# A circulant correlation in a real Fourier basis instead of by skews, a halved last load, and root arithmetic moved to GpSimd

## Chip, cores and metric

The kernel runs on one core of one Trainium2 chip. The metric is device time of one execution in microseconds (us), lower is better. TensorE is called PE below, VectorE DVE, ScalarE ACT, GpSimd POOL and SyncE SP; in the code they are `PE`, `V`, `A`, `G`, `SP`.

## What is computed

Two stages: a cross attention that works by autocorrelation, and a gated FFN whose operands are rounded to FP4 in blocks of 16. Input is x and a context, both 64 x 128 x 256 f32.

```python
def reference(x, ctx, Wq, bq, Wout, bout, w_gate, w_up, w_down):
    h = layernorm(x)
    q, k, v = ((t @ Wq + bq).transpose(0, 2, 1) for t in (h, ctx, ctx))   # 64 x 16 x 128
    corr = real(ifft(fft(q) * conj(fft(k)))).mean((0, 1))                 # 128 lags
    w, lag = top_k(corr, 12); w = softmax(w)
    R3 = sum(w[i] * roll(v, -lag[i], -1) for i in range(12))
    R = broadcast(R3, 16 heads).reshape(64, 128, 256)
    x = x + R @ Wout + bout
    h = layernorm(x)
    g, u = fp4_linear(h, w_gate), fp4_linear(h, w_up)                     # 704 wide
    return x + fp4_linear(silu(g) * u, w_down)
```

`fp4_linear` scales each block of 16 by its largest absolute value over 6, rounds to the FP4 grid and multiplies the rounded operands. As R3 is broadcast over 16 heads and then reshaped, `R @ Wout` has only 4 different blocks of 128 rows, which serve 64 row tiles of x. They are called O[0] to O[3]; each has a 257th column, the mean of its row, for the layernorm that follows.

## The kernel before

**Planner.** Instructions are not issued in the order of the code. `op(engine, cost, function, r=, w=, dl=, ...)` records an operation with what it reads and writes, a cost in ns and a due time `dl`; `Order.emit` works out one order for each engine's queue from the costs and the due times, and issues it. Due times are handed back from an operation to those it needs. The constants at L346 to L376 set the due times: `SLOT` is the length of one FFN tile (5425 ns), `LC` the number of slots by which the down products of a tile may follow its gate and up products, `LEAD` by how many slots the preparation of an x batch runs ahead, `TK`, `TC`, `TO`, `TG`, `TW` the due times of single steps.

**Phase 1 (to about 55 us).** One SP queue loads, in the order of the string `LOADS` (L373): weights, x transposed in sixteen 512 KB pieces (`xt`, into eight buffers that are reused), the context in eight 1 MB blocks (`ct`, five buffers), then Wout (`Wo`) and the bias (`Bo`, broadcast to 128 partitions). DVE and ACT round the FFN weights to FP4 and split each into a high and a low f16 part (`WgH`, `WgL`, `WdH`, `WdL`), transposed by DMA. PE projects x to `qT`, with the layernorm applied behind it, and each context block to `kT` (`pk`, L1053); k and v are the same. For each of the 16 blocks of 128 rows `pg` (L1076) adds kTᵀ qT, a 128 x 128 sum over all batches and channels. Filler products of the identity ("heating", L724) keep PE's clock up where it would stand still.

**From pg to O (54.7 to 66 us).** The correlation at a lag is the sum of a circular diagonal of pg. pg is copied twice side by side to `W` (L1091), and `skew` shifts row p by p in seven predicated copies, each for one bit of p, of W onto itself 64, 32, ... 1 columns to the left (L329 to L341).

A product with ones (L1365) then gives the correlation C, the same on all partitions. `max`, `match_replace`, `max`, `match_replace` (L1387 on) find the 12 largest, `E` (ACT) holds the exponentials, and a masked product gives the weights twice side by side in `M` with their sum `es`. A second skew makes `M` the circulant matrix of the weights. M times Wo (L1441) is `Wp`, divided by `es`; eight pairs of transposes (L1372) with a copy each turn kT into `Vn`, which is v with time on the partitions. For each of four g, three products (bias row, two of Vn and Wp, L1459) make O[g], copied by ACT (L1466). ACT also computes the row means of Wo and Bo, loads the table for Sqrt, and fills the constant end columns of the three h buffers (`least`, L1476).

**Phase 2, the FFN (73.6 us to the end).** There are 64 tiles in 16 x batches of four. `x_parts` (L424 to L651) prepares a batch: row mean `neg`, `cc` = x + O less its mean, squares with a sum (`junk`, L507), block maxima `am` (L517), the reciprocal root of the variance, scaling, rounding (`k`, on ACT) and a split into two f16 parts (`xhl`). From tile 8 on the addition of O to X is a DMA that adds, issued by POOL (L481), and the root is worked out by `roots` (L402 to L422), eleven DVE steps on 128 x 4 or 128 x 8 values: once each for batches 2 and 3, then once per two batches. The step at L550 (it writes `am`) reads the result. The first eight tiles take ACT's Sqrt. Tiles of x are transposed (`xT`) by PE for the first two batches and by DMA after.

`group_ops` (L1140 to L1341) runs one or two tiles: gate and up products `gu` (18 matmuls per tile, L1166), Silu `g` (ACT, L1172), `h` = gate times up (DVE, L1179), block maxima `hs` (DVE, L1189) and their reciprocal (`hr`), the wide product `z` (POOL, L1218; DVE for the first and the last two tiles), rounding `hk`, `hc` (ACT), `hl` (DVE, L1271), a DMA transpose to `hT`, down products `pd` (17 matmuls per tile, L1315 and L1317), the sum with X (L1334) and the output DMA. Before the FFN two of the `gu` accumulators are called `hot` and `pa`.

## Time and profile before

| what | us |
|---|---|
| median of three runs | 439.63 |
| lowest and highest of them | 439.36 and 443.25 |
| the profiled execution | 438.03 |
| its span in the profile | 435.9 |
| last context block waited for until | 51.20 |
| last `pg` product ends | 54.72 |
| first copy of O starts | 66.01 |
| first `gu` product of the FFN starts | 73.57 |
| last `pd` product ends | 432.55 |

The profiled execution is 2.13 us longer than its span, which counts from the first instruction to the last on the engines. The table of stretches gives what each engine did between those marks (columns: stretch, its length, then for each engine busy us and instructions; PEclk is the granted clock as a share of full speed, then the busy share of the DMA engines and GB/s):

```profile
0.00:20.00 20.00, 16.33 (x151) 12.08 (x152) 16.30 (x59) 9.24 (x10) 0.92 (x8) 1.00 0.89 339
20.00:54.72 34.72, 33.26 (x445) 21.38 (x441) 25.31 (x56) 27.22 (x40) 0.00 (x0) 1.00 1.05 389
54.72:73.57 18.85, 14.78 (x87) 11.07 (x87) 14.46 (x52) 10.63 (x36) 1.08 (x2) 1.00 1.07 289
73.57:129.28 55.71, 50.14 (x294) 28.10 (x294) 54.90 (x129) 46.03 (x95) 20.55 (x19) 1.00 0.54 114
129.28:432.55 303.27, 301.40 (x1976) 192.76 (x1976) 277.27 (x537) 193.06 (x307) 114.39 (x94) 1.00 0.67 146
```

Between 73.57 and 129.28 DVE is busy 54.90 of 55.71 us and PE 50.14; from there to 432.55 PE is busy 301.40 of 303.27. Instructions of an engine run in its queue's order, so one that waits holds all that stand behind it.

### The profile page before, as it was taken

The page shows a single profiled execution, that of the slowest core. Times are in us where ns is not written, and L with a number is a line of the kernel's source. Part 1 is how long each engine was busy: PE and PEld are TensorE (multiplying, and loading weights), DVE is VectorE, ACT ScalarE, POOL GpSimd, SP SyncE. Part 2 cuts the span into 40 slices and gives each one's busy share as a digit, 9 for nine tenths or more (in the row PEclk, how much of TensorE's full clock was granted, in tenths as well). Part 3 has the DMA queues.
Part 4 walks back from the last instruction along what each step waited for, and adds up shares of the span by engine and source line. Part 5 has one row for each costly group of instructions (what it writes and reads, how often), then busy time and mean ns, then how long its engine had stood idle before and what let it go on. Part 6 is the DMA issues. An engine that isn't in the chain of part 4 may idle for free.

```text
span 435.9 us, 7976 instructions
## 1 busy us (share of the span) xinstructions
PE 415.9 (95%) x2948; PEld 265.4 (61%) x2948; DVE 388.7 (89%) x832; ACT 286.2 (66%) x484; POOL 136.9 (31%) x121
## 2 busy tenths in 40 slices
PE   7999978889899999999999999999999999999996
PEld 6457655446555656566566666666665666566685
DVE  6999368999999999989999989999999999978872
ACT  2797547988596696467946794887579666464410
POOL 0000003044444264344444444454434222324100
PEclk9999999999999999999999999999999999999999
DMA  7999999253787588579767897687578615952362
GB/s 282 408 415 420 334 215 358 37 105 71 151 185 142 131 196 175 139 117 233 157 136 161 197 158 163 139 176 152 117 161 164 156 39 120 192 125 66 94 169 74
DMA packets 151495, 76.61 MB, mean 176 GB/s; under 512 B 134432, under 2 KB 141984, under 8 KB 150432
## 3 DMA queue, kind: packets, MB, share of 16 engines
q1 hardware_dynamic: 143968, 69.29, 59.5%
q0 software_dynamic: 7488, 6.82, 11.0%
q8 instruction: 23, 0.38, 0.4%
q14 instruction: 16, 0.13, 0.1%
HBM read 27.76 MB, written 8.39 MB: 83 GB/s over the span
## 4 chain that ended last, share of the span: by engine, by line
PE 61%; DVE 16%; DMA 9%; ACT 9%; issue 2%; SPq 1%; DVEq 0%; ACTq 0%
PE gu L1166 37%; PE pd L1315 14%; PE pd L1317 8%; DMA ct<-in_cx_dram 6%; DMA xt<-in_xt_dram 4%; DVE hs L1189 3%; DVE h L1179 2%; DVE hl L1271 2%; ACT junk L507 2%; ACT cc L497 2%; ACT g L1172 2%; DVE am L517 1%; ACT hk L1246 1%; ACT hc L1262 1%; DVE hr L1203 1%
## 5 line engine op out<-in xcount | busy, mean ns | idle before, releaser
L1166 PE MATMUL gu<-WgH,xT 128*128 128x512 f16 (+1 forms) x768 | 191.7, 361 | 5.5 <-ACT g L1172 1.5
L1166 PEld LDWEIGHTS <-xT 128*128 128x128 f16 x1152 | 112.4, 98 | 114.8 <-issue 4.5
L1218 POOL TENSOR_TENSOR h<-h,hr 128x704 f32<-128x704 f32 x61 | 92.8, 1521 | 199.0 <-DVE hr L1203 169.7
L1166 PE MATMUL gu<-WgL,xT 128*128 128x512 f16 (+1 forms) x384 | 107.4, 361 | 0.0
L1172 ACT ACTIVATE g<-gu,ug 128x704 f32<-128x704 f32 x64 | 53.6, 840 | 41.8 <-PE gu L1166 41.6
L1246 ACT ACTIVATE hk<-h,c_half 128x1408 int16<-128x1408 f32 (+1 forms) x34 | 47.4, 1394 | 37.3 <-POOL h L1218 34.5
L1189 DVE TENSOR_REDUCE hs<-h 128x44 f32<-128x792 f32 x64 | 66.7, 1042 | 2.1
L481 POOL DMA_DIRECT2D X<-O x52 | 45.7, 939 | 71.0 <-DMA X<-in_x_dram 71.0
L1179 DVE SCALAR_TENSOR_TENSOR h<-gu,uh,g 128x704 f32<-128x704 f32 x64 | 55.9, 874 | 5.0 <-ACT g L1172 3.2
L1262 ACT ACTIVATE hc<-hk,c_sub 128x1408 f16<-128x1408 int16 (+1 forms) x32 | 45.6, 1426 | 0.5
L1315 PE MATMUL pd<-WdH,hT 128*128 128x256 f16 x352 | 43.7, 273 | 1.2 <-DMA hT<-hl 1.2
L1315 PEld LDWEIGHTS <-hT 128*128 128x128 f16 x352 | 34.3, 98 | 9.5 <-DMA hT<-hl 1.6
L1334 DVE SCALAR_TENSOR_TENSOR X<-pd,ud,X 128x512 f32<-128x512 f32 (+1 forms) x34 | 24.3, 715 | 11.3 <-PE pd L1317 11.3
L497 ACT ACTIVATE cc<-X,neg 128x256 f32<-128x256 f32 x62 | 30.2, 497 | 3.6 <-DVE neg L459 2.9
L1271 DVE TENSOR_TENSOR hl<-hc,hsb 128x1408 f16<-128x1408 f16 (+1 forms) x34 | 28.7, 843 | 0.2
L1271 DVE TENSOR_TENSOR hl<-hc,hsl 128x1408 f16<-128x1408 f16 (+1 forms) x34 | 28.6, 841 | 0.0
L1203 DVE RECIPROCAL hr<-hs 128x44 f32<-128x44 f32 x64 | 26.8, 419 | 0.2
L507 ACT ACTIVATE junk<-cc 128x256 bf16<-128x256 f32 x64 | 25.9, 405 | 1.0 <-DVE cc L470 0.8
L1317 PE MATMUL pd<-WdL,hT 128*128 128x256 f16 x192 | 26.2, 273 | 0.0
L1232 ACT ACTIVATE hsb<-hs 128x176 bf16<-128x176 f32 (+1 forms) x34 | 11.4, 334 | 19.8 <-DVE hs L1189 19.8
L912 ACT ACTIVATE xsq<-xt,shift 128x1024 f32<-128x1024 f32 x16 | 18.1, 1148 | 9.5 <-DVE shift L908 7.0
L584 DVE TENSOR_TENSOR cc<-cc,rz 128x256 f32<-128x256 f32 x64 | 23.3, 418 | 0.1
(215 smaller groups left out, 532.9 us busy)
## 6 DMA issues: line engine op xcount, KB each, us to landing
xt<-in_xt_dram SPq DMA_DIRECT2D x16, 512.0 KB, 8.1
ct<-in_cx_dram SPq DMA_DIRECT2D x8, 1024.0 KB, 11.5
X<-in_x_dram SPq DMA_DIRECT2D x16, 512.0 KB, 4.5
out_dram<-X SPq DMA_DIRECT2D x30, 256.0 KB, 2.3
X<-O POOLq DMA_DIRECT2D x52, 128.0 KB, 2.8
Wg<-in_wgu_dram SPq DMA_DIRECT2D x2, 512.0 KB, 4.5
Wdn<-in_wd_dram SPq DMA_DIRECT2D x1, 704.0 KB, 9.6
hT<-hl SPq DMA_TRANSPOSE x32, 3.3
```

What stands on the lines that cost most here:

```text
L481: lambda i=i: G.dma_start(Xq.t[:, i0 + i], O[g][:, 0:D], accum_op=ALU.add),
L497: lambda i=i: A.activation(T["cc"].t[:, i], Xq.t[:, i0 + i], AF.Identity, bias=T["neg"].t[:, i : i + 1]),
L1166: PE.matmul(pg.t[:, c0:c1], src[:, b], w[:, k, c0:c1], start=(m == 0), stop=(m == 5))
L1172: lambda pg=pg, g=g: A.activation(g.t, pg.t[:, 0:NF], AF.Silu, scale=ug),
L1179: lambda pg=pg, g=g, i=i: V.scalar_tensor_tensor(B["h"].t[:, i, 0:NF], pg.t[:, NF:NG], uh, g.t, ALU.mult, ALU.mult),
L1189: lambda i=i: V.tensor_reduce(B["s"].t[:, i], B["h"].t[:, i].rearrange("p (jj b e) -> p b jj e", b=NB, e=2), AX.XY, ALU.max, apply_absolut ...
L1218: lambda i=i, zv=zv: (V if zv else G).tensor_tensor(per_block(B["h"].t[:, i, 0:NF], NB), per_block(B["h"].t[:, i, 0:NF], NB), spread(B["r" ...
L1246: lambda: A.activation(sub("k"), sub("h")[:, :, 0:NF], AF.Identity, bias=c_half, scale=24.0),
L1262: lambda: A.activation(flat("c"), flat("k"), AF.Identity, bias=c_sub, scale=SUB),
L1271: lambda e=e, part=part: V.tensor_tensor(B["hl"].t[:, 0:nt, e].rearrange("p t (jj n) -> p t jj n", jj=JJ), sub("c").rearrange("p t (jj n) ...
L1315: PE.matmul(pd, hT.t[:, b], WdH[:, :, b], start=(b == 0), stop=False)
L1317: PE.matmul(pd, hT.t[:, b], WdL[:, :, b], start=False, stop=(b == 5))
```

## The change

**Loads and layout.** The context is laid out on the host so that each half block is a run of its own; the last block is loaded as two halves (`c7a`, `c7b`). The bias is one row instead of 128 and is loaded before the context. The host no longer reverses rows of Wo.

**Fourier basis.** In phase 1 a real Fourier basis is computed: `four[:, 0]` and `four[:, 1]` hold cosine and sine of 2πfl/128 (f from the partition, l along the row), by a triangle wave and a polynomial; `four[:, 2]` is the basis B with cosines on partitions 0 to 64 and sines above, `four[:, 3]` its quarter-turned partner J. `wt` holds the weights of the frequencies. PE transposes B and J into `fourT`.

**From pg to O.** Both skews go. pg is copied once to W; the product T = B W (`fourT[:, 0]` as stationary) and two weighted sums along rows (`uv`) give the spectrum of the correlation, and two products with cosine and sine bring C back. `max` to weights stays, with the weights once in `wm`; two weighted sums (`wv`) give their spectrum. Beside that PE computes B and J times Wo (`spec`) and B times Vn (`Va`, copied by ACT). Wp is a combination of B Wo and J Wo with wv as scalars; O[g] = Vaᵀ Wp plus the bias row times `es`, and the copy to O[g] divides by `es`. kT is turned in four groups of four transposes instead of eight of two, all free to go once T is done (`VB = 0` makes them wait for T only). Row means of Wo and Bo go from ACT to DVE. The load of the Sqrt table moves from behind E to behind the first Va copy and the ACT part of Wp.

**Elsewhere.** The `least` fills and nine of the eleven root steps go to POOL (fourteen steps there, for lack of a fused form). `LC`, `LEAD` and one due time of the first xT copies change, and with them the planned order. The two DMA transposes of the gate weights wait for the second half of the last context block.

```diff
...
+    four = res.tile([P, 4, P], F32, name="four")
+    fourT = res.tile([P, 2, P], F32, name="fourT")
...
-    for k in range(7):
-        V.tensor_single_scalar(bits_i[:, k : k + 1], pidx, 64 >> k, ALU.bitwise_and)
-    V.tensor_copy(bits, bits_i)
+    pf, sine, cosine, fr, wt, wt2, nwt = (const.tile([P, 1], F32, name=n) for n in ("pf", "sine", "cosine", "fr", "wt", "wt2", "nwt"))
+    V.tensor_copy(pf, pidx)
+    V.tensor_scalar(sine, pidx, 64.0, None, ALU.is_gt)
+    V.tensor_scalar(cosine, sine, -1.0, 1.0, ALU.mult, ALU.add)
+    V.scalar_tensor_tensor(fr, sine, -64.0, pf, ALU.mult, ALU.add)
+    V.tensor_scalar(wt, fr, 0.0, -1.0 / P, ALU.is_equal, ALU.mult)
+    V.tensor_scalar(wt2, fr, 64.0, -1.0 / P, ALU.is_equal, ALU.mult)
+    V.scalar_tensor_tensor(wt, wt, 2.0 / P, wt2, ALU.add, ALU.add)
+    V.tensor_scalar(nwt, wt, -1.0, None, ALU.mult)
...
-    def skew(W, key, **kw):
...
-    LC = 4.5
+    LC = 5.5
...
+    VB = 0
+    TF = 49000.0
...
+    GT = 180.0
...
-    LEAD = (0.5, 0.5)
+    LEAD = (3.0, 0.0)
...
+    LOADS = "wq bq wg0 wg1 x0 wg2 x1 x2 x3 wd x4 x5 x6 x7 x8 x9 x10 x11 x12 x13 x14 x15 bo c0 c1 c2 c3 c4 c5 c6 c7a c7b wo"
...
-        op("V", 75, lambda: V.tensor_tensor(t, y, y, ALU.mult), r=[by], w=[bt])
-        op("V", 75, lambda: V.tensor_tensor(t, t, v, ALU.mult), r=[bv], w=[bt])
...
+        op("G", GT, lambda: G.tensor_tensor(t, y, y, ALU.mult), r=[by], w=[bt], port=False)
+        op("G", GT, lambda: G.tensor_tensor(t, t, v, ALU.mult), r=[bv], w=[bt], port=False)
+        op("G", GT, lambda: G.tensor_scalar(p, t, -4.2, None, ALU.add), r=[bt], w=[bp], port=False)
+        op("G", GT, lambda: G.tensor_tensor(p, p, t, ALU.mult), r=[bt], w=[bp], port=False)
+        op("G", GT, lambda: G.tensor_scalar(p, p, 7.0, None, ALU.add), r=[], w=[bp], port=False)
+        op("G", GT, lambda: G.tensor_tensor(p, p, t, ALU.mult), r=[bt], w=[bp], port=False)
+        op("G", GT, lambda: G.tensor_scalar(p, p, -7.0, None, ALU.add), r=[], w=[bp], port=False)
+        op("G", GT, lambda: G.tensor_tensor(y, p, y, ALU.mult), r=[bp], w=[by], port=False)
+        op("G", GT, lambda: G.tensor_tensor(t, y, y, ALU.mult), r=[by], w=[bt], port=False)
+        op("G", GT, lambda: G.tensor_tensor(t, t, v, ALU.mult), r=[bv], w=[bt], port=False)
+        op("G", GT, lambda: G.tensor_scalar(t, t, -0.5 / 3.2**2, 1.5, ALU.mult, ALU.add), r=[], w=[bt], port=False)
+        op("G", GT, lambda: G.tensor_tensor(y, t, y, ALU.mult), r=[bt], w=[by], port=False)
+        op("G", GT, lambda: G.tensor_tensor(t, v, y, ALU.mult), r=[bv, by], w=[bt], port=False)
+        op("G", GT, lambda: G.tensor_scalar(t, t, TINY / 4.0 / -3.2, None, ALU.mult), r=[], w=[bt], port=False)
...
-                op("V" if fast else "A", 420 if fast else 590, f_x, r=[pt], w=[(T["xT"], i)], dl=due - 300, port=False)
+                op("V" if fast else "A", 420 if fast else 590, f_x, r=[pt], w=[(T["xT"], i)], dl=due - (4300 if fast else 300), port=False)
...
-            "bo": (400, ["Bo"], lambda: SP.dma_start(Bo[:, 0:D], bo.partition_broadcast(P))),
+            "bo": (60, ["Bo"], lambda: SP.dma_start(Bo[:, 0:D], bo)),
...
+                    lambda j=j, b=b: SP.dma_start(cts[j].t[:, b], cx[j, b]),
...
+        mrow = W
...
+        op("G", 300, lambda: G.iota(ang(), pattern=[[0, 2], [1, P]], base=0, channel_multiplier=0), w=[(scr, "ang")])
+        for k in range(2):
+            op("V", 170, lambda k=k: V.tensor_scalar(ang()[:, k], ang()[:, k], fr, 96.0 * k, ALU.mult, ALU.add), w=[(scr, "ang")], dl=TF)
+        op("V", 300, lambda: V.tensor_single_scalar(ang(), ang(), 127, ALU.bitwise_and), w=[(scr, "ang")])
+        op("V", 220, lambda: V.tensor_scalar(tri(), ang(), -1.0 / 64.0, 1.0, ALU.mult, ALU.add), r=[(scr, "ang")], w=[(scr, "tri")])
+        op("V", 330, lambda: V.scalar_tensor_tensor(tri(), tri(), -1.0, tri(), ALU.mult, ALU.max), w=[(scr, "tri")])
+        op("V", 220, lambda: V.tensor_scalar(tri(), tri(), -0.5, None, ALU.add), w=[(scr, "tri")])
+        op("V", 330, lambda: V.tensor_tensor(tri2(), tri(), tri(), ALU.mult), r=[(scr, "tri")], w=[(scr, "tri2")])
+        op("V", 220, lambda: V.tensor_scalar(poly(), tri2(), SIN[4], SIN[3], ALU.mult, ALU.add), r=[(scr, "tri2")], w=[(scr, "poly")])
+        op("V", 330, lambda: V.tensor_tensor(poly(), poly(), tri2(), ALU.mult), r=[(scr, "tri2")], w=[(scr, "poly")])
+        for k in (2, 1):
+            op("V", 330, lambda k=k: V.scalar_tensor_tensor(poly(), poly(), SIN[k], tri2(), ALU.add, ALU.mult), r=[(scr, "tri2")], w=[(scr, "poly")])
+        op("V", 330, lambda: V.scalar_tensor_tensor(four[:, 0:2], poly(), SIN[0], tri(), ALU.add, ALU.mult), r=[(scr, "poly"), (scr, "tri")], w=["four"])
+        for k in range(2):
+            op("V", 130, lambda k=k: V.tensor_scalar(tri()[:, k], four[:, 1 - k], sine, None, ALU.mult), r=["four"], w=[(scr, "tri")])
+            op(
+                "V",
+                200,
+                lambda k=k: V.scalar_tensor_tensor(four[:, 2 + k], four[:, k], cosine, tri()[:, k], ALU.mult, (ALU.add, ALU.subtract)[k]),
+                r=["four", (scr, "tri")],
+                w=["base"],
+            )
+        op("V", 330, lambda: V.tensor_reduce(Bo[:, D : D + 1], Bo[:, 0:D], AX.X, ALU.add), w=["Bo"], dl=TF)
+        op("V", 75, lambda: V.tensor_scalar(Bo[:, D : D + 1], Bo[:, D : D + 1], 1.0 / D, None, ALU.mult), w=["Bo"], dl=TF)
+        pf_t = r_m.new()
+
+        def f_four():
+            for k in range(2):
+                PE.transpose(pf_t.t[:, k * P : (k + 1) * P], four[:, 2 + k], ident)
+
+        op("PE", 300, f_four, r=["base"], w=[pf_t], dl=TC - 1500.0)
+        op("A", 350, lambda: A.copy(fourT.rearrange("p k n -> p (k n)"), pf_t.t[:, 0 : 2 * P]), r=[pf_t], w=["fourT"], dl=TC - 1000.0)
+        op("V", 220, lambda: V.tensor_copy(W, pg), r=["pg"], w=["W", "mrow"], dl=TC + 4000.0)
...
-    skew(W, "W")
...
-    sums = op("PE", 220, lambda: PE.matmul(hot.t[:, 512 : 512 + P], ones, W[:, 0:P], start=True, stop=True), r=["W"], w=[pc])
...
+    T_op = op("PE", 270, lambda: PE.matmul(C(), fourT[:, 0], W, start=True, stop=True), r=["W", "fourT"], w=[pc])
+    uv_ops = []
+    for k in range(2):
+        uv_op = op(
+            "V",
+            280,
+            lambda k=k: V.scalar_tensor_tensor(jk, C(), wt, four[:, 2 + k], ALU.mult, ALU.mult, accum_out=uv[:, k : k + 1]),
+            r=[pc, "base"],
+            w=["jk", ("uv", k)],
+        )
+        uv_ops.append(uv_op)
+
+    def f_c():
+        for k in range(2):
+            PE.matmul(C(), uv[:, k : k + 1].broadcast_to([P, P]), four[:, k], start=(k == 0), stop=(k == 1))
+
+    sums = op("PE", 540, f_c, r=[("uv", 0), ("uv", 1), "four"], w=[pc])
+    op("V", 600, lambda: V.tensor_reduce(Wo[:, :, D : D + 1], Wo[:, :, 0:D], AX.X, ALU.add), w=["Wo"], after=uv_ops)
+    op("V", 75, lambda: V.tensor_scalar(Wo[:, :, D : D + 1], Wo[:, :, D : D + 1], 1.0 / D, None, ALU.mult), w=["Wo"])
+    pv3 = Q["pd"].new()
+    for j in range(4):
+        key, pv = ((pa, j), pa.t[:, 512 * j : 512 * j + 512]) if j < 3 else (pv3, pv3.t)
 
         def f_v(j=j, pv=pv):
-            for b in range(2):
-                PE.transpose(pv.t[:, b * P : (b + 1) * P], kT[:, 2 * j + b], ident)
-
-        op("PE", 220, f_v, r=[("kT", 2 * j), ("kT", 2 * j + 1)], w=[pv], after=after)
+            for b in range(4):
+                PE.transpose(pv[:, b * P : (b + 1) * P], kT[:, 4 * j + b], ident)
...
+        op("PE", 600, f_v, r=[("kT", 4 * j + b) for b in range(4)], w=[key], after=(T_op,) if j >= VB else ())
...
+    pb1 = Q["pd"].new()
+    spec = {
+        ("B", 0): ((hot, "b0"), lambda: hot.t[:, 512 + P : 512 + P + D + 1]),
+        ("J", 0): ((hot, 2), lambda: hot.t[:, 1024 : 1024 + D + 1]),
+        ("B", 1): (pb1, lambda: pb1.t[:, 0 : D + 1]),
+        ("J", 1): ((hot, "j1"), lambda: hot.t[:, P : P + D + 1]),
+    }
+    for (n, e), (key, t) in spec.items():
+        op(
+            "PE",
+            530,
+            lambda t=t, n=n, e=e: PE.matmul(t(), fourT[:, "BJ".index(n)], Wo[:, e], start=True, stop=True),
+            r=["fourT", "Wo"],
+            w=[key],
+            after=(T_op,),
+        )
+    op("A", 450, lambda: A.copy(JB, spec["J", 0][1]()), r=[(hot, 2)], w=["JB"])
+    quick = []
+    for g in range(4):
+        t = lambda g=g: pa.t[:, 256 * g : 256 * g + 256]
+        op(
+            "PE",
+            530,
+            lambda t=t, g=g: PE.matmul(t(), fourT[:, 0], Vn[:, g].rearrange("p b c -> p (b c)"), start=True, stop=True),
+            r=["fourT", "Vn"],
+            w=[(pa, g // 2)],
+        )
+        va_op = op("A", 350, lambda t=t, g=g: A.copy(Va[:, g], t()), r=[(pa, g // 2)], w=[("Va", g)])
+        quick += [va_op] if g == 0 else []
...
-    op("A", 1300, lambda: A.activation(warm, c_half, AF.Sqrt), w=["tbl"], dl=TO)
...
-    skew(M, "M")
...
+    for k in (1, 0):
+        op(
+            "V",
+            280,
+            lambda k=k: V.scalar_tensor_tensor(jk, wm, (wt, nwt)[k], four[:, k], ALU.mult, ALU.mult, accum_out=wv[:, k : k + 1]),
+            r=["wm", "four"],
+            w=["jk", ("wv", k)],
+        )
+    op("V", 75, lambda: V.reciprocal(inv, es), r=["es"], w=["inv"])
+    op("V", 200, lambda: V.tensor_scalar(Wp[:, 0], JB, wv[:, 1:2], None, ALU.mult), r=["JB", ("wv", 1)], w=[("Wp", 0)])
+    t1_op = op("A", 450, lambda: A.activation(Wp[:, 1], spec["J", 1][1](), AF.Copy, scale=wv[:, 1:2]), r=[(hot, "j1"), ("wv", 1)], w=[("Wp", 1)])
+    op("A", 1300, lambda: A.activation(warm, c_half, AF.Sqrt), w=["tbl"], dl=TO, after=[*quick, t1_op])
+    for e in range(2):
+        key, t = spec["B", e]
+        op(
+            "V",
+            450,
+            lambda e=e, t=t: V.scalar_tensor_tensor(Wp[:, e], t(), wv[:, 0:1], Wp[:, e], ALU.mult, ALU.add),
+            r=[key, ("wv", 0)],
+            w=[("Wp", e)],
+        )
+    for g in range(4):
+        bank = (2, 0, 1, 2)[g]
+        po, pn = (pa, bank), pa.t[:, 512 * bank :][:, 0 : D + 1]
+        Vg = Va[:, g].rearrange("p (b r e) -> p e (b r)", b=16, e=2)
+        op(
+            "PE",
+            530,
+            lambda pn=pn: PE.matmul(pn, es[0:1, 0:1].broadcast_to([1, P]), Bo, start=True, stop=False),
+            r=["Bo", "es"],
+            w=[po],
+        )
+        for e in range(2):
+            op(
+                "PE",
+                530,
+                lambda e=e, pn=pn, Vg=Vg: PE.matmul(pn, Vg[:, e], Wp[:, e], start=False, stop=(e == 1)),
...
-            lambda g=g, pn=pn: A.copy(O[g], pn),
-            r=[po],
+            lambda g=g, pn=pn: A.activation(O[g], pn, AF.Copy, scale=inv),
+            r=[po, "inv"],
...
-    cx_l = c(cx.reshape(4, 8, 256, 2, P).transpose(1, 4, 3, 0, 2))
+    cx_l = c(cx.reshape(4, 8, 2, P, 2, P).transpose(1, 2, 5, 4, 0, 3))
...
-    rev = (-np.arange(P)) % P
-    wo_l = c(wo[:, _PERM_D].reshape(2, P, D)[:, rev].transpose(1, 0, 2))
-    bo_l = c(bo[_PERM_D])
+    wo_l = c(wo[:, _PERM_D].reshape(2, P, D).transpose(1, 0, 2))
+    bo_l = c(bo[_PERM_D].reshape(1, D))
...
```

## Prediction

> **What bounds the kernel now.** I read the page's busy shares and slices first. TensorE (PE) is busy 95% of the span and its granted clock is 9 tenths or more in every slice, so time is lost only where PE's row dips: the first fifth.
>
> ```profile
> PE 415.9 (95%) x2948; PEld 265.4 (61%) x2948; DVE 388.7 (89%) x832; ACT 286.2 (66%) x484; POOL 136.9 (31%) x121
> ...
> PE   7999978889899999999999999999999999999996
> ...
> DVE  6999368999999999989999989999999999978872
> ...
> POOL 0000003044444264344444444454434222324100
> ```
>
> The chain of waits says what those slices wait for: the last context block, the last `pg` product, then a serial chain to O, whose first copy is at 66.01. Only 7.56 us later, at 73.57, does the first FFN matmul start.
>
> ```profile
> 39.85 11.35 DMA ct<-in_cx_dram
> ...
> 53.20 1.55 PE pg L1076 x12
> ...
> 57.77 0.49 PE gu L1365 x2
> ...
> 66.01 0.38 ACT O L1466
> ```
>
> The timeline shows what that chain is made of: DVE idle before the copy of pg, a seven-step skew (its twin on M fills 60.55 to 63.04), PE's f32 pairs.
>
> ```profile
> 54.77 0.42 DVE L1091 COPY Wcor<-pg 128x256 f32<-128x256 f32 x1 [7.38 <-PE pg L1076]
> ...
> 55.23 2.49 DVE L336 COPY_PREDICATED Wcor<-bits,Wcor 128x191 f32<-128x191 uint16 x7
> ...
> 58.09 0.60 PE L1372 MATMUL pd<-ident,kT 128*128 128x128 f32 x4
> ...
> 63.15 1.11 PE L1441 MATMUL pd<-Wo,M 128*128 128x257 f32 x4 [0.80 <-issue]
> ```
>
> The table of stretches (columns: length, then busy time of PE, weight load, DVE, ACT, POOL) splits the FFN: to about 130 DVE has no room and PE does; from 150 on PE has none. POOL has room throughout.
>
> ```profile
> 80.00:90.00 10.00, 7.55 (x46) 4.13 (x44) 9.97 (x21) 9.28 (x19) 0.00 (x0) 1.00 0.12 28
> ...
> 120.00:130.00 10.00, 8.91 (x56) 5.16 (x54) 9.76 (x22) 10.00 (x21) 3.67 (x3) 1.00 0.79 179
> ...
> 150.00:160.00 10.00, 10.00 (x68) 6.45 (x66) 9.93 (x18) 9.34 (x21) 4.92 (x5) 1.00 0.83 189
> ```
>
> PE's own waits from 73 us on are few. From 73.57 to 432.55 PE is idle 7.4 us (358.98 less 351.54 busy): 5.6 of it before 129.28, 1.9 after. That is all the FFN can give back.
>
> ```profile
> PE gu L1166 <- ACT g L1172: 1.5, 2, 1.0
> PE gu L1166 <- DVE h L1179: 1.3, 1, 1.3
> PE pd L1315 <- DMA hT<-hl: 1.2, 1, 1.2
> PE pd L1315 <- DMA Wdn<-hl: 1.1, 1, 1.1
> PE gu L1166 <- ACT xT L635: 1.0, 1, 1.0
> ```
>
> **Part 1, loads and the basis (to the copy of pg).** The eighth context block is waited for until 51.20. It is 1.05 MB at 421 GB/s (38 to 46 us), 2.5 us, so its first half would land 1.25 earlier. But all context runs shrink from 8 to 4 KB; the xt loads, which have 4 KB runs, go at 410 GB/s, so 8.39 MB take 0.6 more. Halves: about 50.5 and 51.8. Bo now comes early and as one row; its queue places cost nothing I can see. PE does not get there sooner: it reached the block at 50.99, and now has the two basis transposes (0.5) more ahead of it and qT some 0.3 earlier: 51.1. Then pk 0.58, two pg blocks 0.5, pk 0.58, six pg blocks 1.6: pg ends at 54.3 instead of 54.72, **0.4 gained** (bounds: 0.3 lost if the smaller runs delay the second half further, 1.2 gained if halves overlap fully).
>
> The basis is some 19 DVE instructions ahead of the copy of pg. Priced by neighbours of their size (128x256 tensor-tensor at 0.34 start to start, 128x128 at 0.2 to 0.28) they are 5 to 6 us. Cover: DVE's 7.38 us idle, and it is not in front of qT, because the D weight steps that stood there go behind it: summing the new order, the fourth qT product ends at 46.3 (46.58 before), and the last LdN at about 52.5. Without that cover each us lands on the path. The iota on POOL waits for a freed xt buffer at about 27.6 and holds DVE's queue by at most a few tenths.
>
> **Part 2, from pg to O.** Counted from the end of pg. Before: the skew puts the sums matmul at +3.05, `max` at +3.64, O's first copy at +11.29. After: copy of pg, memset, one heating pair, then the T matmul at +0.75 (the heating started at +0.53 before). The two uv products (0.36 each, by L1410's 0.46 for twice the width) would end at +1.9. But PE has eight transposes queued between T and the C product, 0.24 each by the heating row (18 instructions, nine pairs, 2.17): C starts at +2.95 and `max` at +3.5. So the first skew is **not** won; eight transposes stand in its place. From `max` to the weights is unchanged, 1.73. Then PE is the bound: eight transposes 1.95, B0, J0, J1, first Va product, B1, bias row, two Wp products, each 0.49 (L1459: six instructions 1.59): C ends +3.4, and +1.95 +3.9 gives +9.3. Beside it: E +5.25, weights +5.65, wv +6.0 and +6.5, Wp on DVE +6.95 to +8.35, and on ACT Wp1, Va0 and the Sqrt table load (1.28+0.2) from +7.8 to +9.3. O's first copy at +9.4, that is 63.7: **2.3 gained** together with part 1. PE's queue, DVE's and ACT's table load arrive within 0.2 of each other; if any of them slips, so does O. X0 has landed by then and X1 by about 67.3, wanted at 70.
>
> From O to the first FFN matmul the DVE order is the old one, 7.56: first matmul at 71.2. Two Va copies now stand among ACT's, where DVE's X add covers them.
>
> **Part 3, the ramp.** Here the gain is eaten. ACT: copies of O2 and O3 come after the Silu load, behind three Wp products (1.5 us of PE, moved between tile 0 and 1), and all of k for tiles 4 to 7 before g: the xT copies of tile 2 end at 82.6 where PE started that tile at 82.83. DVE: I summed the start-to-start rows that stand ahead of each h. For before this gives 80.9, 87.5, 98.3, 108.8, 115.2, 128.5 for tiles 0, 1, 4, 6, 7, 9; the trace has 81.18, 87.75, 98.29, 108.76, 115.14, 128.42, so the method holds and DVE is gapless. In the new order the sums are longer by 1.2, 0.8, 2.2 and 1.7 us for tiles 0, 1, 4, 6 (an X add, one `am` and four `cc` products come earlier) and shorter by 1.5 and 3.9 for 7 and 9. With DVE and ACT starting 2.3 earlier, and ACT's waits: 81.0, 87.6, 99.8, 109.9, 113.1, 123.9. PE walked through with 3.57 per gu and 1.86 per pd: idle 2.0 before tile 2, 2.4 before tile 3, 0.2, 1.2 before tile 6, none from there: 5.8. The three DMA waits go, since xhl and hl of these tiles are done 3 to 8 us before PE asks.
>
> Roots: nine of eleven DVE steps per batch become fourteen on POOL. DVE's queue loses about 1.3 us per batch (100.14 to 102.2, less the other work in between), 3.9 by 141 and 10 in all; beyond 130 PE covers that and it is worth nothing. No small arithmetic row on POOL exists; the nearest are the iota and the wide product:
>
> ```profile
> 0.98 0.12 POOL L300 IOTA pidx<- 128x1 int32 x1
> ...
> L1218 POOL TENSOR_TENSOR h<-h,hr 128x704 f32<-128x704 f32 x61 | 92.8, 1521 | 199.0 <-DVE hr L1203 169.7
> ...
> L1218 DVE TENSOR_TENSOR h<-h,hr 128x704 f32<-128x704 f32 x3 | 2.7, 889 | 0.0
> ...
> L421 DVE SCALAR_TENSOR_TENSOR y<-t,y 128x8 f32<-128x8 f32 (+1 forms) x8 | 1.3, 162 | 0.2
> ```
>
> So between 0.12 and 1.52 each; I take 0.2, by the iota, to which eight elements are nearest, with a wait. Fourteen are 2.8 us. DVE's `am` step (L550) now waits for the last; queued behind it are every h and hl. In the first batch the chain starts near 87 and has one z product and one DMA issue (1.47+0.87) in between; DVE asks at 95.8: room up to 0.46 each. Second batch 0.44, third 0.35. It also delays z and X<-O behind it by 2.8 at most, with POOL 36% busy. The `least` fills move from ACT (1.3) to POOL, in its idle start; nothing waits until tile 0's reduce.
>
> The Trainium skill (GPSIMD Engine Reference, Engine selection) says that elementwise work belongs on VectorE, GpSimd being about twice as slow for two inputs. The two L1218 rows show 1.7. By the rule alone the move loses; leaving the roots where they were would put 3.9 us back on DVE in the ramp. What decides is that DVE is full there and POOL is not, which the rule does not weigh.
>
> The later deadlines of pd and the leads change priorities, all inside the order I summed. The tail is the old order: ten pd, transposes, pd.
>
> **The sum** against the profiled execution: first matmul -2.3, moved Wp products +1.5, PE idle 5.8 plus 0.8 later (one g wait of two) against 7.4: -0.8. Total -1.6: span 434.3 for 435.9, execution 436.4 for 438.03, and from the median 439.63: **438.0**.
>
> **Rivals.** (a) The head start is handed on: ACT's copies slip in without holding tile 2, and DVE's 3.9 us of roots come off PE's 5.6 idle. For it: DVE 9.97 of 10 at 80 to 90. Against: the longer sums ahead of tiles 0 to 6. 439.6-2.3-3.9 = 433.4. Chance 0.20. (b) Slower: POOL's steps cost more than 0.46 with their waits, and DVE stands at L550. At 0.7 each, fourteen are 9.8, and the first two batches hold DVE by 3.3 and 3.6 where nothing covers it: 438.0+7 = 445. Against: the iota's 0.12. Chance 0.11. (c) The chain to O is not shorter, because C waits for PE and a handoff more costs what the M skew saved; the ramp's longer sums then cost: about 440.5. Chance 0.09. The forecast keeps 0.60, with its own range 435.8 to 440.2 (unknown of part 1, and 1.5 us in the ramp).
>
> A measurement here tells 1% from no change, 4.4 us. Faster by more than that is (a) and a little of the forecast, 0.22; slower is (b), 0.11; the rest 0.67. The range leaves out half of (a)'s lower side and (b): 433.2 to 441.8.
>
> **What would show it.** O's first copy near 63.7 and `max` +3.5 after pg; transposes back to back ahead of C; first L1166-type matmul near 71.2; h of tile 1 no earlier than 87 although everything before it is; PE idle 5 to 7 us in the FFN; POOL root steps near 0.2 and no DVE idle put down to POOL. Wrong would be DVE idle at the `am` step behind POOL, DVE still busy when pg ends, or h of tiles 0 and 1 two us earlier.

## The result, and the profile after

The changed kernel takes 441.45 us (median of 20 executions, 439.27 to 443.75), the kernel before 439.37 us in 20 (437.80 to 443.25). The ratio is 1.0049 with an interval of 1.0029 to 1.0069: slower by half a per cent. The forecast was 438.0 us and a small gain. The time lies inside its range (433.2 to 441.8), the direction was wrong. The profiled execution took 442.84 us, its span is 441.0.

Marks of that execution, beside the forecast and the profile before, in us (the forecast of the last product is its span of 434.3 less the 3.35 that followed it before):

| | before | forecast | after |
|---|---|---|---|
| last `pg` product ends | 54.72 | 54.3 | 54.33 |
| `max` starts | 58.36 | 57.8 | 57.14 |
| first copy of O | 66.01 | 63.7 | 64.14 |
| first `gu` product | 73.57 | 71.2 | 74.26 |
| PE idle from there to 130 | 5.57 | 5.8 | 4.13 |
| PE idle from 130 on | 1.88 | 0.8 | 5.25 |
| last `pd` product ends | 432.55 | 430.9 | 437.71 |

Two lines of the page after, the busy times and the granted clock over forty slices of 11.0 us:

```profile
PE 419.8 (95%) x2940; PEld 267.1 (61%) x2940; DVE 387.4 (88%) x775; ACT 285.6 (65%) x477; POOL 171.9 (39%) x237
...
PEclk9999996999999999999999999999999999999999
```

POOL has 35 us more to do, DVE 1.3 less. The seventh slice (66 to 77 us) is new: PE got 6 tenths of its clock there, right at the start of the FFN. The table of stretches shows it closer (columns as before the prediction; the clock is the third number from the end):

```profile
64.00:66.00 2.00, 0.97 (x4) 0.47 (x4) 1.28 (x4) 0.85 (x2) 0.00 (x0) 1.00 1.02 209
66.00:68.00 2.00, 1.54 (x4) 0.95 (x5) 1.24 (x3) 1.37 (x6) 0.00 (x0) 0.75 1.02 416
68.00:70.00 2.00, 1.92 (x5) 1.01 (x3) 1.68 (x6) 0.44 (x3) 0.00 (x0) 0.50 1.03 412
...
74.00:76.00 2.00, 2.00 (x7) 0.74 (x6) 1.97 (x6) 1.49 (x6) 1.55 (x2) 0.50 0.49 94
76.00:78.00 2.00, 2.00 (x8) 0.82 (x7) 1.97 (x5) 1.92 (x7) 0.00 (x0) 0.69 0.00 0
```

In half-microsecond stretches the clock is 0.50 from 67.0 to 70.4 and from 73.9 to 77.2. In the second spell a pair of `gu` products takes 0.85 us from start to start instead of 0.43, for some 3.3 us; the first one doubles the products of O1 (2.08 for four, 1.03 before). Between O's first copy and the first `gu` product lie 10.12 us where the forecast kept the old 7.56. ACT's timeline shows the beginning of that, first before, then after:

```profile
66.01 0.37 ACT L1466 COPY O<-gu 128x257 f32<-128x257 f32 x1 [1.68 <-PE gu L1459]
67.20 0.42 ACT L507 ACTIVATE junk<-cc 128x256 bf16<-128x256 f32 x1 [0.81 <-DVE cc L470]
```

```profile
64.14 0.48 ACT L1547 ACTIVATE O<-gu,inv 128x257 f32<-128x257 f32 x1 [0.78 <-PE gu L1463]
65.41 0.37 ACT L1467 COPY Va<-gu 128x256 f32<-128x256 f32 x1 [0.79 <-PE gu L1463]
66.56 0.37 ACT L1467 COPY Va<-gu 128x256 f32<-128x256 f32 x1 [0.79 <-PE gu L1532]
66.83 0.42 ACT L508 ACTIVATE junk<-cc 128x256 bf16<-128x256 f32 x1
```

And PE's timeline after, beside it:

```profile
64.67 0.70 PE L1463 MATMUL gu<-Vn,fourT 128*128 128x256 f32 x2 [0.57 <-ACT O L1547]
65.83 0.69 PE L1532 MATMUL gu<-Bo,es 1*128 1x257 f32 x2 [0.46 <-ACT Va L1467]
```

The squares of the first tile (`junk`) start 2.69 after O's copy, where it was 1.19. They stand on ACT behind two copies of Va, and ACT and PE take turns there: by the profile's releasers a product on PE waits for O's copy, the first copy of Va for that product, a bias row on PE for that copy, and the second copy for the bias row, 0.79 for each copy. After 130 us PE waits again and again, mostly for `g`:

```profile
PE gu L1196 <- ACT g L1202: 3.2, 5, 1.0
PE gu L1196 <- DVE h L1209: 1.1, 2, 0.7
PE pd L1345 <- DMA Wdn<-hl: 0.9, 1, 0.9
```

The kernel before waited 1.5 us there, all for `g`.

Executions of one kernel differ by their mean granted clock. In every profile of this case in which the clock falls while PE has work, it falls to 0.50, for 3.4 us or a multiple of that. The profiles with one such spell have a mean clock of 0.995 or 0.996, those with two 0.992, the one with three 0.988, the one with four 0.985. The kernel before took 437.6 to 438.5 us at a clock of 0.998 or more, mostly 439.2 to 439.9 at 0.991 or 0.992 (two spells), and 441.1 to 443.1 at 0.988 or less. The changed kernel took 439.27 to 440.88 at 1.000, 440.68 to 442.66 at 0.995 or 0.996, and 442.62 to 443.75 at 0.988 to 0.992. Its profile has two spells, the profile of before has none. So a difference of the two profiles, 4.8 us, overstates that of the medians, 2.08. But the clock is not what made the change lose: at full clock alone (medians 439.78 and 438.03) it is still 1.75 slower.

### The profile page after: what moved, and what is told of

Read it like the earlier page. It is cut to its first block, busy times and chain, and to the rows that moved or that the text cites. A ratio compares the mean times of both kernels' runs of the same rounds, so it can differ in the third digit from the quotient of the medians.

```text
span 441.0 us, 7983 instructions
## 1 busy us (share of the span) xinstructions
PE 419.8 (95%) x2940; PEld 267.1 (61%) x2940; DVE 387.4 (88%) x775; ACT 285.6 (65%) x477; POOL 171.9 (39%) x237
## 4 chain that ended last, share of the span: by engine, by line
PE 51%; DVE 18%; ACT 11%; DMA 9%; issue 5%; POOL 4%; SPq 1%; ACTq 0%; POOLq 0%; DVEq 0%
PE gu L1196 27%; PE pd L1345 11%; PE pd L1347 6%; DMA xt<-in_xt_dram 4%; DVE hl L1301 3%; DVE hs L1219 3%; DVE h L1209 3%; POOL h L1248 2%; ACT cc L498 2%; ACT junk L508 2%; DVE xhl L614 2%; ACT hk L1276 2%; ACT g L1202 2%; DMA Wg<-in_wgu_dram 1%; DMA X<-O 1%
## 5 line engine op out<-in xcount | busy, mean ns | idle before, releaser
L482 POOL DMA_DIRECT2D X<-O x52 | 46.7, 936 | 50.6 <-ACT junk L508 44.2
L599 ACT ACTIVATE k<-cc,c_half 128x1024 int16<-128x1024 f32 (+1 forms) x16 | 17.9, 1117 | 7.9 <-DVE cc L585 7.9
```

Of the source, the lines that this page charges most:

```text
L482: lambda i=i: G.dma_start(Xq.t[:, i0 + i], O[g][:, 0:D], accum_op=ALU.add),
```

## The experiments

All times are medians, and ratios are to the kernel before on the same chip. A ratio is not the quotient of two medians: those of e8_due_only give 0.996, its ratio is 0.9989. The marks and the idle time are those of one profiled execution each; changed and e1_heat, which have one order, differ by 0.47 in the last column. Idle is PE's, in the FFN, ahead of and from 130 us on.

| kernel | us | ratio | O copy | first gu | idle to 130 | idle from 130 |
|---|---|---|---|---|---|---|
| before | 439.37 | | 66.01 | 73.57 | 5.57 | 1.88 |
| changed | 441.45 | 1.0049 (1.0029 to 1.0069) | 64.14 | 74.26 | 4.13 | 5.25 |
| e1_heat | 439.58 | 1.0005 (0.9985 to 1.0025) | 64.04 | 72.79 | 4.22 | 4.78 |
| e5_va_behind | 439.66 | 1.0024 (1.0000 to 1.0048) | 63.94 | 71.81 | 3.78 | 5.12 |
| e2_roots_dve | 442.34 | 1.0072 (1.0046 to 1.0097) | 63.73 | 73.36 | 6.55 | 2.50 |
| e3_due_old | 448.71 | 1.0215 (1.0187 to 1.0243) | 63.80 | 72.57 | 10.71 | 4.03 |
| e6_chain_heat | 443.80 | 1.0110 (1.0083 to 1.0137) | 64.26 | 74.08 | 6.17 | 4.85 |
| e4_roots_only | 442.88 | 1.0080 (1.0050 to 1.0111) | 67.68 | 75.24 | 4.57 | 6.10 |
| e8_due_only | 437.59 | 0.9989 (0.9961 to 1.0017) | 66.26 | 73.82 | 4.84 | 1.57 |
| e9_roots_due | 442.46 | 1.0079 (1.0055 to 1.0102) | 66.71 | 74.27 | 6.67 | 3.33 |
| e13_pool_idle_steps | 447.25 | 1.0188 (1.0148 to 1.0229) | 67.89 | 75.45 | 6.49 | 6.03 |
| e12_same_order | 440.27 | 1.0020 (0.9999 to 1.0041) | 64.19 | 72.94 | 5.28 | 3.53 |
| e10_gt290 | 439.85 | 1.0014 (0.9993 to 1.0035) | 64.07 | 72.81 | 5.49 | 2.73 |
| e11_sum | 439.30 | 1.0011 (0.9996 to 1.0025) | 63.76 | 72.00 | 5.74 | 2.14 |
| e14_before_heat | 438.67 | 0.9993 (0.9978 to 1.0009) | 66.21 | 73.77 | 4.37 | 2.06 |
| e15_mended | 438.57 | 0.9996 (0.9981 to 1.0012) | 63.83 | 72.06 | 5.81 | 2.39 |
| e16_due_heat | 437.71 | 0.9977 (0.9961 to 0.9993) | 66.92 | 74.48 | 5.11 | 1.43 |

The theories: S, the loss is ahead of the FFN (clock, and the copies of Va); R, the root steps on POOL disturb the FFN; L, the new due times do.

**Fillers in the changed kernel (e1_heat).** `warm_pe(n)` issues n products of the identity into `hot`. They sit in the functions of the planned operations, so the plan and the order of the others do not change.

```diff
-            lambda t=t, g=g: PE.matmul(t(), fourT[:, 0], Vn[:, g].rearrange("p b c -> p (b c)"), start=True, stop=True),
+            lambda t=t, g=g: (PE.matmul(t(), fourT[:, 0], Vn[:, g].rearrange("p b c -> p (b c)"), start=True, stop=True), warm_pe(2 if g else 0)),
...
-            lambda pn=pn: PE.matmul(pn, es[0:1, 0:1].broadcast_to([1, P]), Bo, start=True, stop=False),
+            lambda pn=pn, g=g: (PE.matmul(pn, es[0:1, 0:1].broadcast_to([1, P]), Bo, start=True, stop=False), warm_pe(1 if g == 1 else 0)),
```

> The changed kernel with seven filler products (0.24 us each) put behind the Va products and one bias row, where PE stood still between 64 and 70 us; every queue's order is otherwise that of the changed kernel. Theory S-clock (half of the loss is the granted clock of 0.50 from 67 to 70 and 74 to 77 us): clock 1.00 throughout, O1's products take 1.0 instead of 2.1 us, the first gu products 0.43 instead of 0.85 apart, time about 2 us less than the changed kernel, ratio to the kernel before about 1.000. Theory L or R (the loss is the idle after 130 us, from due times or from roots on POOL): ratio stays near 1.005.

The same stretches of this kernel:

```profile
64.00:66.00 2.00, 1.86 (x12) 1.43 (x11) 1.38 (x4) 0.85 (x2) 0.00 (x0) 1.00 0.95 192
66.00:68.00 2.00, 1.96 (x9) 1.34 (x9) 1.15 (x3) 1.47 (x6) 0.00 (x0) 1.00 1.01 401
68.00:70.00 2.00, 1.88 (x12) 1.30 (x11) 1.76 (x6) 1.80 (x7) 0.00 (x0) 1.00 1.03 420
...
74.00:76.00 2.00, 2.00 (x12) 0.98 (x10) 1.93 (x8) 1.97 (x8) 1.57 (x3) 1.00 0.53 109
```

PE is busy where it stood still, the clock stays at 1.00, and `gu` starts 1.47 earlier. Ten of twelve executions have a clock of 0.999 or more. The median falls by 1.87: shown. At full clock the times are those of the changed kernel at full clock (439.25 to 439.92 here), so the gain of the fillers is one of the clock. Idle after 130 is 4.78, so something else is left.

**Copies of Va behind the squares (e5_va_behind).**

```diff
+        later += [va_op] if g else []
...
+    n0 = len(S.ops)
     for i, n, e in FIRST:
         x_stage(R4, 0, i, n, True, TG + i * STEP0, e, True, True)
+    for o in later:
+        o.after.update(u for u in S.ops[n0:] if u.eng == "A")
```

> The changed kernel with the ACT copies of Va 1 to 3 held behind the squares and roots of the first two tiles. Theory S-queue (those copies stand ahead of the squares on ACT and wait for PE, which waits for O's copy): the squares start at about 65.4 instead of 66.83, first gu product at about 72 instead of 74.26, ratio about 1.000. Rival (the ramp eats any head start, as forecast): first gu earlier by 2, h of tile 1 not earlier, ratio 1.003 to 1.006.

ACT's timeline here:

```profile
63.94 0.48 ACT L1548 ACTIVATE O<-gu,inv 128x257 f32<-128x257 f32 x1 [0.78 <-PE gu L1463]
65.23 0.42 ACT L508 ACTIVATE junk<-cc 128x256 bf16<-128x256 f32 x1 [0.81 <-DVE cc L471]
```

The squares now wait only for `cc`, and `gu` starts at 71.81, 7.87 after O's copy. This profile is at full clock, so the queue is to be judged against e1_heat, where it took 8.75 with the copies in front: the queue cost 0.88, and the other 1.37 of the 10.12 went with the clock. Five of twelve executions still have a clock of 0.996 or less, which holds the median up. But `h` of tile 1 comes at 88.43, against 88.51 with the fillers, whose `gu` starts one us later: that part of the rival holds.

**Roots back on DVE, and old due times (e2_roots_dve, e3_due_old).** The first puts the eleven DVE steps back, the second is:

```diff
-    LC = 5.5
+    LC = 4.5
-    LEAD = (3.0, 0.0)
+    LEAD = (0.5, 0.5)
...
-                op("V" if fast else "A", 420 if fast else 590, f_x, r=[pt], w=[(T["xT"], i)], dl=due - (4300 if fast else 300), port=False)
+                op("V" if fast else "A", 420 if fast else 590, f_x, r=[pt], w=[(T["xT"], i)], dl=due - 300, port=False)
```

> The changed kernel with the eleven root steps back on DVE. Theory R (roots on POOL upset the order after 130 us): PE idle after 130 us falls from 5.2 to about 2, ratio 0.998 to 1.000. Theory S or L: idle after 130 stays at 4 or more, DVE has 3.9 us more to do before 130 and PE idles more there, ratio 1.005 to 1.013.

> The changed kernel with LC 4.5, LEAD (0.5, 0.5) and the old due time of the first xT copies. Theory L (the new due times make the idle after 130 us): PE idle after 130 falls from 5.2 to about 2, ratio 0.998 to 1.000. Theory S or R: idle after 130 stays at 4 or more, ratio 1.003 to 1.008.

With the roots on DVE idle from 130 on falls from 5.25 to 2.50, as R has it; idle before 130 rises from 4.13 to 6.55, one stall of 4.25 behind xT among it, and the time does not fall. With the old due times, L expected a gain; there is a loss outside of all that was expected. The waits of PE say what it is:

```profile
PE gu L1196 <- DMA xT<-xhl: 7.4, 1, 7.4
PE gu L1196 <- ACT g L1202: 4.2, 5, 1.6
```

One batch of x is prepared 7.4 us too late, and the clock is at 0.50 for three spells behind that wait (117.3 to 127.5). L falls: the new due times are what makes the rest bearable.

**Parts alone (e6_chain_heat, e4_roots_only, e8_due_only, e9_roots_due).** The basis with the old roots and due times and the fillers of e1; the kernel before with the roots on POOL; with `LC = 5.5`, `LEAD = (3.0, 0.0)` and the new xT due time; and with both.

> Basis, loads and least fills of the change, with root steps on DVE and the due times of before, and the seven fillers that keep the clock. Theory (the three parts of the change are worth something only together): the ramp of the kernel before returns, PE idle before 130 about 5.6 and after 130 about 2, first gu product at 72.8, so span 0.8 shorter than before: ratio 0.998. Rival (each part costs by itself, the chain too): ratio above 1.003.

> The kernel before with the fourteen root steps on POOL, all else as before. Theory R (roots on POOL make the idle after 130 us, and need the new due times, or xT of batch 2 or 3 comes too late): one stall of several us of gu behind the DMA of xT near 115 to 122, idle after 130 about 5 instead of 1.9, ratio 1.015 to 1.022. Rival (the fault lies between the new chain and the old due times): no such stall, DVE's 3.9 us gained before 130, ratio 0.993 to 0.998.

> The kernel before with LC 5.5, LEAD (3.0, 0.0) and the new due time of the first xT copies. Theory R: idle after 130 stays near 1.9, ratio 1.000 to 1.006 (batches 2 and 3 are prepared earlier and push h). Theory L (the due times make the idle after 130): idle there near 5, ratio 1.005 to 1.010.

> The kernel before with the root steps on POOL and the new due times: the second half of the change alone. Theory R with L: no long stall behind xT, idle before 130 about 4 (of 5.6), after 130 about 5 (of 1.9): ratio 1.002 to 1.006. Rival (the two parts gain by themselves and only the chain costs): ratio 0.994 to 0.998.

The basis without its due times loses 1.1%, as the rival had it: a batch again comes late (2.9 us of waiting for xT, 2.7 for `xhl`), and fillers at one place did not keep the clock (0.992). The roots alone lose 0.8%, where R expected 1.5 to 2.2; the long stall that R expected near 115 to 122 is 0.68 there and 1.62 at 162, and the gain before 130 (5.57 to 4.57) is there too, but idle from 130 on is 6.10. Roots with due times lose as much (0.8%, more than expected), with 6.67 before 130. The due times alone are no worse than before: 437.59 us, with an interval that includes 1, and idle from 130 on of 1.57. In each of the three pairs that differ in the roots alone (e2 and changed, before and e4, e8 and e9) idle from 130 on is higher by 1.8 to 4.2 with the roots on POOL. (e6 and e3, which differ in the fillers too, go the other way, 4.85 and 4.03; 2.70 of e6's are the one late `xhl`.)

**Steps that nobody reads (e13_pool_idle_steps).** The kernel of e8_due_only, its roots on DVE, and for each batch:

```diff
+    def idle_steps(n):
+        d = dum[:, 0:n]
+        for m in range(14):
+            G.tensor_scalar(d, d, 1.0, None, ALU.mult) if m in (2, 4, 6, 10, 13) else G.tensor_tensor(d, d, d, ALU.mult)
```

> The kernel before with the new due times (437.59 us, idle after 130 of 1.57 us), and beside each batch of roots on DVE fourteen small POOL steps on a tile of their own, which nobody reads; the order of every other queue is the same. Theory Q (the root steps hurt because the wide products z stand behind them in POOL's queue): z waits up to 2 us behind hr once or twice per batch, PE idle after 130 rises from 1.6 to 3 or 4, 1 to 3 us more than that kernel. Theory C (they hurt because the root's own chain takes 4 us instead of 2): no change, idle stays at 1.6.

Nothing waits for these results, and the kernel is 9.7 us slower by the medians of the two comparisons (447.25 for 437.59). Part of that is the clock, as all its executions have 0.992 or less; at 0.992 the two kernels took 444.94 and 445.20 for 437.62 to 438.74, some 7 more. In the profile, two spells at 61.0 to 67.8 and 1.63 of delay up to the first `gu` come before the first of these steps (76.8), and so are not theirs. The worst place, first POOL, then ACT, then PE:

```profile
179.07 0.48 POOL L408 TENSOR_TENSOR dum<-dum 128x8 f32<-128x8 f32 x2
179.63 0.23 POOL L408 TENSOR_SCALAR dum<-dum 128x8 f32<-128x8 f32 x1
179.83 1.52 POOL L1226 TENSOR_TENSOR h<-h,hr 128x704 f32<-128x704 f32 x1
```

```profile
181.39 1.47 ACT L1254 ACTIVATE hk<-h,c_half 128x1408 int16<-128x1408 f32 x1 [4.17 <-POOL h L1226]
182.76 0.83 ACT L1180 ACTIVATE g<-gu,ug 128x704 f32<-128x704 f32 x1
```

```profile
183.64 0.65 PE L1174 MATMUL gu<-WgH,xT 128*128 128x384 f16 x2 [2.86 <-ACT g L1180]
```

The wide product `z` stands behind the small steps, 2.57 after its `hr`. ACT waits 4.17 with `hk`, the last 2.4 of them by this delay; `g` of the next tile stands behind `hk`, and PE waits 2.86 for `g`. A spell of half clock follows (183.8 to 187.2). So the way from small steps to PE that theory Q names is shown, at this place. The whole price is more than Q's 1 to 3 us: five of 61 `z` come 0.5 to 2.57 late, and idle rises by 4.46 from 130 on, of which this wait is 2.86, and by 1.65 before. From the timelines of DVE and POOL, `z` starts 0.09 to 0.22 us behind `hr` in 60 of 61 cases before (0.45 once); in the changed kernel twelve wait longer, up to 1.87, 11.0 us more in sum (20.56 for 9.57). But there the late `z` meet few of PE's waits: of the eight from 130 on one (0.26 at 149.33) comes within 10 us of a late `z`, and the three long ones for `g` (0.96 at 219.39, 0.98 at 289.67, 0.88 at 348.48) do not. Whether a delay is handed on over more than one tile is not shown.

**Same plan, other engine, and a truer price (e12_same_order, e10_gt290).** In the first the planner still books the steps on POOL, and their functions issue the nine DVE instructions; in the second `GT` is 290 instead of 180. Both have the fillers of e1.

> The changed kernel with fillers (439.58 us, idle after 130 of 4.78 us), with the root steps run by DVE as nine instructions at the places where POOL had them in the plan; the order of PE, ACT and SP is the same. Theories Q and C (POOL's execution): idle after 130 falls to 2 or 3, but DVE gets its 1.7 us per batch back and idle before 130 rises by up to 3.9; total within 1 us of that kernel. Theory O (the planned order, not POOL, makes the idle): idle after 130 stays near 4.8 or grows, total 1 to 4 us more.

> The changed kernel with fillers, with the planner told 290 ns per root step on POOL (their measured spacing) instead of 180. Theory P (the planner puts z too early because it thinks POOL free 1.5 us before it is): idle after 130 falls from 4.8 to 2 or 3, ratio to the kernel before 0.995. Otherwise: idle stays at 4 or more, ratio near 1.000.

Without POOL in it but the same order, no `z` waits, and idle from 130 on falls from 4.78 to 3.53, between the theories: about 1.3 us are POOL's execution, 1.7 above the 1.88 of before are in the planned order, as far as single profiles show it. The wait of 0.87 for `g` at 345 is there too, without any late `z`. With the true spacing in the plan idle from 130 on falls to 2.73, as P has it, but idle before 130 grows by 1.3, and the ratio is not the 0.995 expected. At a clock of 1.000 that kernel took 437.88 to 438.63 us, e1_heat 439.25 to 439.92. So a good part of the fault is a price of 180 ns for what takes 290. It is not the order alone: `z` waits less as well, 12.41 in sum for 21.45 in e1_heat.

**Sums (e11_sum, e14_before_heat, e15_mended, e16_due_heat).** e11_sum is the change with fillers, e5's order and roots on DVE; e15_mended keeps the roots on POOL at 290 ns. e14 and e16 put five fillers behind transposes of kT in the kernel before and in e8_due_only:

```diff
                 PE.transpose(pv.t[:, b * P : (b + 1) * P], kT[:, 2 * j + b], ident)
+            for _ in range({1: 2, 7: 3}.get(j, 0)):
+                PE.matmul(hot.t[:, 0:P], ident, ident, start=True, stop=True)
```

> What the runs so far speak for, together: basis, loads, least fills and new due times of the change, root steps on DVE, fillers, and the ACT copies of Va 1 to 3 behind the squares of the first tiles. If head start and due times add up: first gu product at 71.8, full clock, idle of FFN 6.4 as with the due times alone, 1.2 of PE for moved Wp products: last pd at 431, 436.2 us, ratio 0.993. If the ramp eats the head start (a stall behind the DMA of xT near 115, 4 us with roots on DVE before): ratio 0.998 to 1.003.

> The kernel before with five fillers (0.24 us each) where PE stood still between its copy of pg and its Wp products; every queue's order is otherwise the same. Theory K (executions differ by how many spells of half clock fall into 55 to 75 us: 438.0 us at a mean clock of 0.999, 439.5 at 0.992, 442.8 at 0.985): nearly all executions at a clock of 0.996 or more, median 438.0 to 438.5, ratio 0.996 to 0.998. Rival (the clock follows the length of the wait, not PE's idle time): the same three groups, median 439.4.

> All parts of the change, with fillers, 290 ns per POOL root step in the plan, and the ACT copies of Va 1 to 3 behind the squares. If the three mended faults are what made the change slower: first gu product at 71.9, idle in the FFN about 8, full clock: 437.0 us, ratio 0.994 to 0.997. If the ramp gives the head start back: 438.0 to 438.6 as with the 290 ns alone at full clock.

> The kernel before with the new due times and the same five fillers: no basis, no roots on POOL. Theory K: 436.8 us in nearly all executions, ratio 0.993 to 0.995. Rival: groups as without fillers (436.9 to 442.5), median 437.6.

e11_sum is the second of its two cases: `gu` at 72.00, but a stall of 3.15 behind xT at 115, and a ratio of 1.0011. In e14 the spells become fewer and move: the profile has one at 73 to 77, eight of twelve executions have a clock of 0.995 and three 0.999; 438.67 us for 439.17 in that comparison, with an interval that includes 1. So theory K holds for the groups, but not for the price: the median is above its 438.0 to 438.5, and fillers in one place only move part of the spells. e15_mended, with the three faults mended and all parts of the change kept, has a clock of 1.000 in eleven of twelve executions and takes 438.57 us: like the kernel before, not better, the second of its two cases. The due times with fillers (e16), without basis and without roots on POOL, are the only version whose interval lies below 1: 0.9961 to 0.9993. Theory K's 436.8 us did not come; the 437.71 is the median that its rival gave, and six of twelve executions still have a clock of 0.992.

## Why the prediction was wrong

**pg and the chain to O: right, with two sizes off.** pg ended at 54.33 (54.3 forecast). The basis cost nothing visible: DVE stood idle 2.39 before the copy of pg. `max` came 2.81 after pg, not 3.5: the eight transposes of kT ahead of C, where the forecast put 0.24 each by the filler row, took 0.13 each.

```profile
55.26 1.04 PE L1426 MATMUL gu<-ident,kT 128*128 128x128 f32 x8
```

The trace has sixteen instructions for the sixteen transposes of kT, one each, while the product for T has two (L1401, x2), and a filler too; the forecast had taken the price of a pair. From `max` to O's copy it was 7.0 instead of 5.9: two products on PE waited 0.46 and 0.47 for ACT (for E, which had itself waited 0.50 for a product, and for the copy JB). The forecast had added up PE's work there without waits. O came 0.44 later than forecast, 1.87 earlier than before.

**From O to the first FFN product: wrong, the first failed step.** The step read "the DVE order is the old one, 7.56" and "two Va copies now stand among ACT's, where DVE's X add covers them". The copies, 0.37 us each, were put at nothing. What they cost is what they wait for: they stand on ACT in front of the squares, and each waits 0.79 for PE, which itself waits for ACT. It took 10.12 us; at full clock 8.75 with the copies in front (e1) and 7.87 behind (e5), so of the 2.56 by which the term was too small 0.88 are the queue's, 1.37 came with the clock, and 0.31 are left in e5. The start of `gu` was forecast 2.4 earlier and came 0.7 later.

**The clock: missing in the prediction.** It read "granted clock is 9 tenths or more in every slice" as a property of the kernel. It was one of one execution: 34 of 104 executions of the kernel before in four comparisons have 0.998 or more, 58 have 0.991 or 0.992. So the changed kernel does not have more spells than before, but each costs more: at full clock, with one spell and with two its medians are 439.78, 441.26 and 442.9, while the two spells of the kernel before cost it 1.44 together. Where they fall in that kernel no profile of it shows. In e4_roots_only and e13, whose code up to the FFN is almost the same, two lie at 60.0 to 67.8, where PE waits for the chain; in the changed kernel one lies in the FFN. Fillers give 1.87 us back (e1). Of the 3.06 by which the first `gu` was late, 1.47 are of this kind.

**The ramp: right in the main.** With full clock (e1_heat) `h` of tiles 0, 1, 4, 6 and 7 come at 82.10, 88.51, 100.80, 110.87 and 114.07; the forecast was 81.0, 87.6, 99.8, 109.9 and 113.1. That is 0.9 to 1.1 late throughout, and tile 9 is 1.8 late. The late start of `gu` is not why: in e5, with `gu` 0.98 earlier than in e1, `h` of tile 1 comes 0.08 earlier. Idle before 130 is 4.22 for 5.8, the moved products cost 1.23 for 1.5. The head start is eaten as forecast.

**Roots on POOL: the second failed step.** The price was too low. A step takes 0.20 undisturbed, as forecast, but the next one starts 0.29 after it, and some steps last as long as a DVE instruction beside them (the mean of all 112 is 0.29). Fourteen were put at 2.8; those from 110.22 to 115.60, with nothing between them, took 5.38. Rival (b) did not come even so: DVE waits at `am` for POOL 0.2 us in all. What failed is the effect on the rest of the FFN. The text said of the queue behind the steps "it also delays z and X<-O behind it by 2.8 at most, with POOL 36% busy", and priced it at nothing, and of the gain "beyond 130 PE covers that". A mean share of 36% says nothing of fourteen steps in a row. PE was idle 4.78 to 5.25 from 130 on where 0.8 was forecast, and 1.8 to 4.2 more than with the roots on DVE in three pairs of kernels. The Trainium skill's advice that the prediction weighed (GPSIMD Engine Reference, Engine selection: elementwise work belongs on VectorE) came out right for the roots alone, 1.0080 in e4. It is not the whole of it: with 290 ns in the plan the roots on POOL (e15_mended, 0.9996) are no worse than on DVE (e11_sum, 1.0011). e13 shows one way in which small steps reach PE, without any gain from the roots; in the changed kernel e12 points to the planner's order as the larger part (1.65 of 2.90 more idle, from single profiles), and with 290 ns in the plan (e10) 2.05 of it go, though 1.27 come back before 130.

Put together, at full clock (e1_heat against the profile before): first `gu` -0.78, moved products +1.23, idle before 130 -1.35, idle after +2.90, in sum 2.0 later at the last product. The forecast had -2.37, +1.5, +0.23 and -1.08, in sum 1.7 earlier. So of the 3.7 that it missed at full clock idle after 130 is 4.0 and the start of `gu` 1.6, less 1.9 by which the ramp came better. The clock comes on top in most executions. With the three faults mended (e15_mended) the loss is gone, and the forecast gain does not come: its last product ends at 432.79, 0.24 later than before. What stays open is which of the orders after 130 makes the last 0.5 us of idle in e15_mended, and whether the due times alone gain and why; no run splits `LC` from `LEAD`.

## What to carry to other kernels

Small instructions that are moved to an idle engine can be paid by the large one behind them in that queue: look at what follows them there, and at who stands behind the waiter, not at the engine's mean share. A copy that is short is not cheap where it waits: price an instruction in front of a critical one by when its input is ready. A half-clock spell costs more in a dense stage than where TensorE waits anyway; fillers can keep the clock up at their place, and the granted clock is to be read from many executions, not from one. Where an order is planned from costs, give a moved instruction its measured spacing, not its duration.
